# PSUM place of the one-hot products, the sums of w1, the logits, the gated additions and the gates' load in a gated expert block

## The chip, the cores and the metric

The kernel runs on one core of a Trainium2 chip. The metric is the device time of one execution in microseconds (us), lower is better. Before the change it is 282.3 us, the median of three runs (282.22 to 282.58).

A core has five engines with a queue each: PE (TensorE, matrix products into PSUM), DVE (VectorE), ACT (ScalarE), POOL (GpSimd) and SP (SyncE, which here only issues DMAs). Each engine works through its queue in order, and waits where an instruction needs what another engine has not finished.

## The reference

Two gated blocks over x, which has 2048 tokens of 512 numbers. The first sends each token through the one of four experts that its id names; all three matrices of an expert are the same 512x512 matrix. The second is a feed-forward of three layers whose result is added up by routes.

```
x = x + tanh(g_xattn) * xattn(layernorm(x))
x = x + tanh(g_ffn) * ffn(layernorm(x))

xattn(h): e = min(clip(id) // 6250, 3);  y = (silu(h @ C_e.T) * (h @ C_e.T)) @ C_e
ffn(h):   p = softmax(h @ wr.T);  i1, i2 = top_2(p);  gates = p[i] / sum(p[i])
          v = silu(silu(h @ w1.T) @ w3.T) @ w2.T
          out[i_k[t]] += gates[t, k] * v[t]
```

The routes are row numbers from 0 to 7, so the second block changes only the first eight rows of the output: all tokens' v, weighted, are summed into them.

## The kernel before

**Passes.** The tokens are sorted by expert and packed into 17 passes of 128 rows; 13 passes have one expert, four ("shared" passes) have four groups of 32 rows, each with an expert matrix of its own. `order` fixes their sequence, in which the shared passes are the 7th, 11th, 14th and 17th. The place of each token comes from counts that are taken on the chip: `idt` is loaded and compared with the experts' bounds, TensorE counts (`cnt`), DVE works out places, and 16 products of one-hot matrices (`atlane` and `what`) give `tok`, the number of the token at each place (lines 276 to 280). `from_row` and `to_row` are read off `tok` by DVE: the first at once (line 307), the second in `row_tables` (lines 316 and 317), which stands in DVE's queue after the first pass's norms and before the first pass's `g` (line 475). `busy` fills TensorE's waits with products nobody reads.

**One pass.** `gather` (POOL, an indirect DMA) brings 128 rows of x; `load` (SP) brings the expert's matrix of 1 MB, whose number SP first reads from the table `which`; `centre` and `scale` norm the rows on DVE; `turn_in` transposes them on TensorE (`tp_a`) and ACT copies the result; `up` is the first product (z), ACT's Silu and DVE's product (line 475) make `g`; `turn_mid` transposes g (`tp_g`); `down` is the second product (y), which DVE adds to x (line 489) with `tg`, the tanh of the gates; POOL scatters the rows to the output. `norms` norms them again for the feed-forward (small DVE steps on 128x1 and then `h_f`, line 513), `turn_out` transposes them (`tp_f`) into `hT2`.

**The feed-forward.** It runs over two blocks of 1024 rows. The first layer multiplies w1 by hT2 in Strassen's way with seven products in place of eight, and needs sums of parts of w1 (`sums_of_w1`, lines 589 to 592, on POOL) and of hT2 (`sums_of_hT`, on DVE), which also issues the `logits` and transposes them (`turned`). `route` finds the two largest logits and writes the gates `g`, on a tile that POOL clears (line 577). `second_layer(b, g)` covers a quarter of 512 rows: for each of four tiles the product v (line 734), then ACT's Silu into `s2`; then the four additions `acc` (line 746), each a product of a 32-column part of g with s2 into a 32-row part of one PSUM bank. The quarters are numbered 0 to 3. For the last the order is another, since its end is the kernel's end.

**What sets the order.** The program is written in the order in which each engine runs it; nothing reorders it. The main loop (lines 863 to 893) issues pass i's first product, pass i-1's second and pass i-2's last transposes. The feed-forward is a Python generator that issues a piece of work at each `yield`; `step()` takes the next piece, two or so in each pass of the loop, and after the loop all the rest. So TensorE's queue mixes the passes' products with pieces of the feed-forward.

**PSUM and buffers.** There are eight banks: two for tag "mm" (cnt, idle, tok, z, y, v), two for tag "x" (lg and X), one for Y, two for transposes (`tp`), one for the sums (`acc`). A tile of a tag takes the buffer of the one two before it, once that has been read for the last time. Of SBUF, the tiles named in `on_the_way` lie in a pool that is closed after `row_tables`, and its room is used again by the feed-forward's tiles.

Of the kernel before, what the change touches and what calls it, by code (L numbers as in the profile page):

```python
# [8 lines left out]
F32 = mybir.dt.float32  # L9
# [4 lines left out]
AF = mybir.ActivationFunctionType  # L14
# [5 lines left out]
P = 128  # L20
# [5 lines left out]
def tile_gated_moe_ffn(  # L26
# [40 lines left out]
    nc = tc.nc  # L67
# [6 lines left out]
    NP = NJ + 1  # L74
# [4 lines left out]
    NB = NT // TB  # L79
    HB = TB // 2  # L80
    TT = HB // P
# [14 lines left out]
    pos = positions.enter_context(tc.tile_pool(name="pos", bufs=1))  # L96
    on_the_way = {
        "lane", "atlane12", "atlane4", "passes", "what", "place", "over", "rank_in", "incl",
        "keep", "cum", "hot", "before", "later", "stepped", "behind",
    }  # L100

    def ct_(shape, dtype, name):
# [5 lines left out]
    idt = ct_([P, NJ], I32, "idt")  # L108
    nc.sync.dma_start(idt, ids)
    gates = ct_([P, 2], F32, "gates")  # L110
    nc.scalar.dma_start(gates[:, 0:1], g_xattn.to_broadcast([P, 1]))
    nc.scalar.dma_start(gates[:, 1:2], g_ffn.to_broadcast([P, 1]))

    def load_w(src, name):
        w = ct_([P, KC, src.shape[1]], F32, name)
# [62 lines left out]
    for e in range(NR):  # L178
        nc.gpsimd.memset(rank[:, :, e : e + 1], float(NR - e))
    tg = ct_([P, 2], F32, "tg")  # L180
    nc.scalar.activation(tg, gates, AF.Silu)
    nc.scalar.activation(tg, gates, AF.Tanh)


    nc.vector.tensor_tensor(
# [87 lines left out]
        what, what, number.unsqueeze(1).to_broadcast([P, NP, NJ]), ALU.mult  # L273
    )
    at_lane(1)
    tok = ps_mm.tile([P, NP], F32, tag="mm", name="tok")
    for j in range(NJ):
        nc.tensor.matmul(
            tok, atlane[j // H][:, :, j % H], what[:, :, j], start=(j == 0), stop=(j == NJ - 1)
# [158 lines left out]
    def load(p):  # L438

        n0, n = (p, 1) if p < NF else (NF + (p - NF) * G, G)  # L440
        mats[p] = []
        for i in range(n0, n0 + n):
            at = nc.values_load(
                early[i] if i in early else which[0:1, i : i + 1],
                engines=[SP],
                min_val=0,
                max_val=(E - 1) * D,
                skip_runtime_bounds_check_because="an expert's number, times D",
            )
            m = mp.tile([P, KC, D], F32, tag="m", name=f"m_{i}")  # L450
            nc.sync.dma_start(m, ctxT[bass.ds(at, D), :].rearrange("(k p) f -> p k f", p=P))
            mats[p].append(m)
# [130 lines left out]
    def sums_of_w1():  # L583

        h = D // 2
        a11, a12 = w1[:, 0:2, 0:h], w1[:, 2:4, 0:h]
        a21, a22 = w1[:, 0:2, h:D], w1[:, 2:4, h:D]
        ss = [ffp.tile([P, 2, h], F32, tag=f"S{i}", name=f"S{i}") for i in range(1, 5)]
        nc.gpsimd.tensor_add(ss[0], a21, a22)
        nc.gpsimd.tensor_sub(ss[1], ss[0], a11)  # L590
        nc.gpsimd.tensor_sub(ss[2], a11, a21)
        nc.gpsimd.tensor_sub(ss[3], a12, ss[1])
        return a11, a12, a22, ss

    def sums_of_hT(b):

# [128 lines left out]
    def second_layer(b, g):  # L725

        c_b = b % 2 * HB

        def gated(t, half=None):

            c0, n = (0, D) if half is None else (half * D // 2, D // 2)
            v = ps_mm.tile([P, n], F32, tag="mm", name=f"v_{b}_{t}_{c0}")
            for k in range(KC):
                nc.tensor.matmul(  # L734
                    v,
                    s1[:, k, c_b + t * P : c_b + (t + 1) * P],
                    w3[:, k, c0 : c0 + n],
                    start=(k == 0),
                    stop=(k == KC - 1),
                )  # L740
            s2 = work.tile([P, n], F32, tag="s2", bufs=4, name=f"s2_{b}_{t}_{c0}")
            nc.scalar.activation(s2, v, AF.Silu)  # L742
            return s2

        def add(t, s2):
            nc.tensor.matmul(  # L746
                acc[t * Q : (t + 1) * Q, :],
                g[:, t, :],
                s2,
                start=(b == 0),  # L750
                stop=(b == NH - 1 if t < TT - 2 else b == NH - 2),
            )

        def add_turned(t, k, s2):

            nc.tensor.matmul(  # L756
                accT[:, k, :],
                s2,
                g[:, t, 0:NR],
                start=(t == TT - 2 and k == 0),  # L760
                stop=(t == TT - 1 and k == KC - 1),
                skip_group_check=True,
            )

        s2s = []
        if b < NH - 1:
            for t in range(TT):
                s2s.append(gated(t))
                yield
            for t in range(TT):  # L770
                add(t, s2s[t])
            yield SHORT
            return
        for t in range(TT - 1):
            s2s.append(gated(t))
            yield
        for t in range(TT - 2):
            add(t, s2s[t])
        a = work.tile([P, D], F32, tag="g", bufs=2, name="a")
        nc.scalar.copy(a, acc)  # L780
        half0 = gated(TT - 1, 0)
        for k in range(KC):
            add_turned(TT - 2, k, s2s[TT - 2][:, k * P : (k + 1) * P])
        tp = transposed(a, "sum")
        nc.vector.tensor_reduce(
            aT[:, :, 0:NR],
            tp.rearrange("p (k t q) -> p k q t", k=KC, t=TT)[:, :, 0:NR, :],
            AX.X,
            ALU.add,
        )  # L790
        def finish(i, s2):
            n = KC // 2
            for k in range(n):
                add_turned(TT - 1, i * n + k, s2[:, k * P : (k + 1) * P])
            ks = slice(i * n, (i + 1) * n)
            nc.vector.tensor_add(aT[:, ks, 0:NR], aT[:, ks, 0:NR], accT[:, ks, :])

        finish(0, half0)
        half1 = gated(TT - 1, 1)
        out_product(0, KC // 2)  # L800
        finish(1, half1)
# [17 lines left out]

    SHORT = 1  # L820
    last = {b: max(i for i, p in enumerate(order) if min(p // (TB // P), NB - 1) == b) for b in range(NB)}
    running, hT_sums, lts = [], {}, {}

    def step():
        if running:
# [13 lines left out]
    for i in range(1, 5):  # L839
        gather(order[i])  # L840
    load(order[1])
    first_in(order[0])
    centre(order[1])
    scale(order[0], order[1])
# [11 lines left out]
    up(order[1], inside=lambda: turn_mid(order[0]))  # L856
    turn_in(order[2])
    centre(order[3])
    down(order[0])
    turn_mid(order[1])  # L860
    norms(order[3], order[0])
    load(order[4])
    for i in range(2, NP + 2):
        if i < NP:
            up(order[i])
        if i + 1 < NP:
            turn_in(order[i + 1])
        if i + 2 < NP:
            centre(order[i + 2])
        if i + 3 < NP:  # L870
            gather(order[i + 3])
            load(order[i + 3])
        if i <= NP:
            down(order[i - 1])
        else:
            step()
        turn_out(order[i - 2])
        if i <= NP:
            norms(order[i + 2] if i + 2 < NP else None, order[i - 1])
        step()  # L880
        for b in range(NB):
            if last[b] == i - 2:
                hT_sums[b] = sums_of_hT(b)
                running.append(ffn(b))
        if i == 4:
            w1_sums = sums_of_w1()
        if i == 7:
            w3 = load_w(w3T, "w3")
            w2 = load_w(w2T, "w2")
        if i < NP:  # L890
            turn_mid(order[i])
        if last[0] != i - 2:
            step()
    fetched = False
# [52 lines left out]
```

## Time and profile before

| what | value |
|---|---|
| median of three runs | 282.3 us |
| profiled execution | 284.29 us |
| its span (first to last instruction) | 282.6 us |
| granted TensorE clock | 1.0 of full |
| TensorE, a 128x512 f32 product of v, records each | 570 ns, starts 0.43 us apart |
| DVE, T's sums, 128x1024 f32 | 1.22 us |
| POOL, w1's sums, 128x512 f32, four | 1.27 to 1.30 us each |
| ACT, Silu of v, 128x512 | 0.60 us |

The profile comes from one execution, so its span is set against its own 284.29 us. Records of one engine's matrix products overlap[...]: what a product costs is the distance between starts, not a record's length, and "PE busy" can be high where TensorE is held up. In the timeline a row has start, length, engine, line, operation, output and inputs, shape, count, and in brackets the idle time before it with what ended it.

### The profile page before, as it was taken

How to read it: one execution, taken by the hardware profiler on the slowest of the kernel's cores; microseconds unless marked ns; L12 is line 12 of the kernel's file. 1: busy time of each engine (PE TensorE's matmuls, PEld its weight loads, DVE VectorE, ACT ScalarE, POOL GpSimd, SP SyncE). 2: the span in 40 equal slices, each digit the busy share in tenths (PEclk: the TensorE clock that was granted, in tenths of full speed). 3: DMA queues.
4: the chain of work that ended last, by engine and by line, in shares of the span. 5: the costliest groups of instructions: out<-in, count | busy, mean ns of one | idle time of the engine just before them, and what ended most of it. 6: DMA issues, size and time to landing. Idle time of an engine off the chain costs nothing.

```text
span 282.6 us, 3568 instructions
## 1 busy us (share of the span) xinstructions
PE 270.3 (96%) x1173; PEld 126.3 (45%) x1173; DVE 149.0 (53%) x592; ACT 69.5 (25%) x134; POOL 44.3 (16%) x66
## 2 busy tenths in 40 slices
PE   4978999999999999999999999999999999999994
PEld 1434555544445445444444354534345544443463
DVE  4378777799777669935534382506350711620000
ACT  2022213313313321323315132312113224211120
POOL 5420122282222112311101010101010000000000
PEclk9999999999999999999999999999999999999999
DMA  0686999556649998397515085001000000000000
GB/s 1 195 288 196 376 393 382 211 199 224 202 146 396 392 394 333 103 355 258 179 31 186 2 248 232 37 0 39 0 11 0 3 1 0 0 0 2 0 0 2
DMA packets 20722, 42.54 MB, mean 151 GB/s; under 512 B 2143, under 2 KB 2207, under 8 KB 20704
## 3 DMA queue, kind: packets, MB, share of 16 engines
q1 hardware_dynamic: 17664, 33.66, 34.1%
q0 software_dynamic: 2720, 8.65, 8.4%
q8 instruction: 9, 0.15, 0.2%
q14 instruction: 9, 0.07, 0.1%
q10 hardware_dynamic: 320, 0.01, 0.1%
HBM read 38.10 MB, written 4.47 MB: 151 GB/s over the span
## 4 chain that ended last, share of the span: by engine, by line
PE 87%; DVE 7%; DMA 3%; issue 1%; ACT 0%; ACTq 0%; POOL 0%; DVEq 0%
PE y L461 20%; PE v L734 20%; PE z L461 19%; PE X L626 10%; PE Y L626 5%; PE tp_g L388 3%; PE tp_f L388 3%; PE Z L626 2%; PE tp_a L388 2%; DMA x<-in_x_dram,from_row 2%; PE acc L746 1%; DMA idt<-in_ids_dram 1%; PE lg L703 1%; DVE q_f L369 1%; PE accT L756 1%
## 5 line engine op out<-in xcount | busy, mean ns | idle before, releaser
L461 PE MATMUL z<-m,hT 128*32 128x512 f32 (+1 forms) x232 | 61.8, 595 | 2.1 <-DVE pads L320 1.9
L461 PE MATMUL y<-m,gT 128*32 128x512 f32 (+1 forms) x232 | 61.4, 594 | 0.0
L734 PE MATMUL v<-w,s 128*128 128x512 f32 (+1 forms) x136 | 57.0, 570 | 0.0
L734 PEld LDWEIGHTS v<-w,s 128*128 128x128 f32 x136 | 25.1, 190 | 28.2 <-issue 26.8
L461 PEld LDWEIGHTS z<-m,hT 128*32 128x32 f32 (+1 forms) x232 | 22.6, 146 | 31.3 <-issue 27.9
L461 PEld LDWEIGHTS y<-m,gT 128*32 128x32 f32 (+1 forms) x232 | 22.5, 146 | 27.9 <-issue 27.9
L490 POOL DMA_INDIRECT out_dram<-x,to_row x17 | 17.1, 1008 | 90.9 <-DVE x L489 89.0
L397 POOL DMA_INDIRECT x<-in_x_dram,from_row x17 | 16.9, 995 | 72.3 <-DVE h_a L409 29.9
L475 DVE SCALAR_TENSOR_TENSOR g<-z,rs_a,g 128x512 f32<-128x512 f32 x17 | 12.7, 748 | 27.4 <-ACT g L474 27.4
L474 ACT ACTIVATE g<-z,rs_a 128x512 f32<-128x512 f32 x17 | 11.7, 688 | 49.4 <-PE z L461 48.9
L489 DVE SCALAR_TENSOR_TENSOR x<-y,tg,x 128x512 f32<-128x512 f32 x17 | 12.7, 749 | 19.4 <-PE y L461 19.4
L742 ACT ACTIVATE s<-v 128x512 f32<-128x512 f32 (+1 forms) x17 | 9.7, 572 | 44.0 <-PE v L734 44.0
L523 ACT COPY hT<-tp_f 128x512 f32<-128x512 f32 x13 | 7.6, 586 | 43.4 <-PE tp_f L388 43.4
L626 PE MATMUL X<-T,S 128*128 128x512 f32 x32 | 15.0, 592 | 0.0
L348 DVE BATCH_NORM_STATS2 st_a<-x 128x6 f32<-128x512 f32 x16 | 11.0, 686 | 6.6 <-DMA x<-in_x_dram,from_row 6.6
L388 PEld LDWEIGHTS tp_f<-ident,h_f 128*128 128x128 f32 x68 | 8.1, 141 | 11.0 <-issue 9.7
L481 ACT COPY gT<-tp_g 128x512 f32<-128x512 f32 x17 | 10.0, 586 | 12.5 <-PE tp_g L388 12.4
L348 DVE BATCH_NORM_STATS2 st_f<-x 128x6 f32<-128x512 f32 x17 | 11.8, 694 | 0.6
L388 PEld LDWEIGHTS tp_a<-ident,h_a 128*128 128x128 f32 x64 | 7.7, 141 | 9.5 <-issue 9.3
L644 DVE TENSOR_TENSOR s<-X,c 128x512 f32<-128x512 f32 x4 | 2.8, 692 | 16.2 <-PE X L626 16.2
L388 PE MATMUL tp_f<-ident,h_f 128*128 128x128 f32 x68 | 10.5, 276 | 0.6 <-DVE h_f L513 0.6
L388 PE MATMUL tp_g<-ident,g 128*128 128x128 f32 x68 | 10.5, 275 | 0.2
(164 smaller groups left out, 281.6 us busy)
## 6 DMA issues: line engine op xcount, KB each, us to landing
m<-in_ctxT_dram SPq DMA_DIRECT2D x29, 1024.0 KB
w<-in_w1T_dram SPq DMA_DIRECT2D x1, 1024.0 KB
w<-in_w3T_dram SPq DMA_DIRECT2D x1, 1024.0 KB
w<-in_w2T_dram SPq DMA_DIRECT2D x1, 1024.0 KB
x<-in_x_dram,from_row POOLq DMA_INDIRECT x17, 6.3
out_dram<-x,to_row POOLq DMA_INDIRECT x17, 6.0
wr<-in_wrT_dram SPq DMA_DIRECT2D x1, 64.0 KB
x_first<-out_dram SPq DMA_DIRECT2D x4, 4.0 KB
```

The lines of the kernel that those rows point to most:

```text
L348: nc.vector.bn_stats(st, xt)
L388: nc.tensor.transpose(tp[:, k * P : (k + 1) * P], h[:, k * P : (k + 1) * P], ident)
L397: nc.gpsimd.indirect_dma_start(out=xt, out_offset=None, in_=x, in_offset=bass.IndirectOffsetOnAxis(ap=from_row[:, p : p + 1], axis=0),)
L461: nc.tensor.matmul(out_ps[i * n : (i + 1) * n, :], lhs[:, k * P + i * n : k * P + (i + 1) * n], m[:, k, :], start=(k == 0), stop=(k == KC ...
L474: nc.scalar.activation(g, z, AF.Silu, scale=rs)
L475: nc.vector.scalar_tensor_tensor(g, z, rs, g, ALU.mult, ALU.mult)
L481: nc.scalar.copy(gT, tp)
L489: nc.vector.scalar_tensor_tensor(xt, y, tg[:, 0:1], xt, ALU.mult, ALU.add)
L490: nc.gpsimd.indirect_dma_start(out=out, out_offset=bass.IndirectOffsetOnAxis(ap=to_row[:, p : p + 1], axis=0), in_=xt, in_offset=None, bou ...
L626: nc.tensor.matmul(out_ps, a[:, k, c * P : (c + 1) * P], bb[:, k, :], start=start and k == 0, stop=k == 1, skip_group_check=True,)
L734: nc.tensor.matmul(v, s1[:, k, c_b + t * P : c_b + (t + 1) * P], w3[:, k, c0 : c0 + n], start=(k == 0), stop=(k == KC - 1),)
L742: nc.scalar.activation(s2, v, AF.Silu)
```

## The change

- `tok` is taken from the two banks of tag "x" and not from those of tag "mm".
- The gates are loaded on SP's queue, after the matrix of the second pass, and not on ACT's at the program's start. ACT's first instruction, which also loads its function table, reads a tile of ones; the Tanh of the gates comes after the copy of the third pass's transposes.
- The four sums of w1 are issued on DVE, one at the end of each of the loop's rounds 5 to 8, after `norms`, and not together on POOL in round 4.
- `sums_of_hT`, with the logits, is issued after `turn_mid` in a round and not before. This moves the first block's logits behind `tp_g`.
- A quarter's four additions are kept in `owed` and issued after the first v of the next quarter (`pay`). `s2` has five buffers and not four.
- In the last round the piece of the feed-forward that stood before the last `turn_out` comes after it, so the last `tp_f` runs before the second quarter's last v.
- Nine more small tiles lie in the pool that is closed early.

On TensorE the instructions are the same ones, in another order; DVE has four more, POOL four fewer, ACT two DMA issues fewer and SP two more.

```diff
--- before.py
+++ after.py
@@ -96,7 +96,8 @@
     pos = positions.enter_context(tc.tile_pool(name="pos", bufs=1))
     on_the_way = {
         "lane", "atlane12", "atlane4", "passes", "what", "place", "over", "rank_in", "incl",
-        "keep", "cum", "hot", "before", "later", "stepped", "behind",
+        "keep", "cum", "hot", "before", "later", "stepped", "behind", "ones", "place0", "number",
+        "idt", "pad", "psum", "padded", "lanes", "inpass",
     }
 
     def ct_(shape, dtype, name):
@@ -108,8 +109,6 @@
     idt = ct_([P, NJ], I32, "idt")
     nc.sync.dma_start(idt, ids)
     gates = ct_([P, 2], F32, "gates")
-    nc.scalar.dma_start(gates[:, 0:1], g_xattn.to_broadcast([P, 1]))
-    nc.scalar.dma_start(gates[:, 1:2], g_ffn.to_broadcast([P, 1]))
 
     def load_w(src, name):
         w = ct_([P, KC, src.shape[1]], F32, name)
@@ -178,8 +177,7 @@
     for e in range(NR):
         nc.gpsimd.memset(rank[:, :, e : e + 1], float(NR - e))
     tg = ct_([P, 2], F32, "tg")
-    nc.scalar.activation(tg, gates, AF.Silu)
-    nc.scalar.activation(tg, gates, AF.Tanh)
+    nc.scalar.activation(tg, ones_f[:, 0:2], AF.Silu)
 
 
     nc.vector.tensor_tensor(
@@ -273,7 +271,7 @@
         what, what, number.unsqueeze(1).to_broadcast([P, NP, NJ]), ALU.mult
     )
     at_lane(1)
-    tok = ps_mm.tile([P, NP], F32, tag="mm", name="tok")
+    tok = ps_x.tile([P, NP], F32, tag="x", name="tok")
     for j in range(NJ):
         nc.tensor.matmul(
             tok, atlane[j // H][:, :, j % H], what[:, :, j], start=(j == 0), stop=(j == NJ - 1)
@@ -586,11 +584,15 @@
         a11, a12 = w1[:, 0:2, 0:h], w1[:, 2:4, 0:h]
         a21, a22 = w1[:, 0:2, h:D], w1[:, 2:4, h:D]
         ss = [ffp.tile([P, 2, h], F32, tag=f"S{i}", name=f"S{i}") for i in range(1, 5)]
-        nc.gpsimd.tensor_add(ss[0], a21, a22)
-        nc.gpsimd.tensor_sub(ss[1], ss[0], a11)
-        nc.gpsimd.tensor_sub(ss[2], a11, a21)
-        nc.gpsimd.tensor_sub(ss[3], a12, ss[1])
-        return a11, a12, a22, ss
+        w1_sums.extend((a11, a12, a22, ss))
+        nc.vector.tensor_add(ss[0], a21, a22)
+        yield
+        nc.vector.tensor_sub(ss[1], ss[0], a11)
+        yield
+        nc.vector.tensor_sub(ss[2], a11, a21)
+        yield
+        nc.vector.tensor_sub(ss[3], a12, ss[1])
+        yield
 
     def sums_of_hT(b):
 
@@ -738,7 +740,7 @@
                     start=(k == 0),
                     stop=(k == KC - 1),
                 )
-            s2 = work.tile([P, n], F32, tag="s2", bufs=4, name=f"s2_{b}_{t}_{c0}")
+            s2 = work.tile([P, n], F32, tag="s2", bufs=5, name=f"s2_{b}_{t}_{c0}")
             nc.scalar.activation(s2, v, AF.Silu)
             return s2
 
@@ -751,6 +753,12 @@
                 stop=(b == NH - 1 if t < TT - 2 else b == NH - 2),
             )
 
+        def pay():
+
+            for f, t, s2 in owed:
+                f(t, s2)
+            owed.clear()
+
         def add_turned(t, k, s2):
 
             nc.tensor.matmul(
@@ -766,13 +774,15 @@
         if b < NH - 1:
             for t in range(TT):
                 s2s.append(gated(t))
+                if t == 0:
+                    pay()
                 yield
-            for t in range(TT):
-                add(t, s2s[t])
-            yield SHORT
+            owed.extend((add, t, s2s[t]) for t in range(TT))
             return
         for t in range(TT - 1):
             s2s.append(gated(t))
+            if t == 0:
+                pay()
             yield
         for t in range(TT - 2):
             add(t, s2s[t])
@@ -819,7 +829,7 @@
 
     SHORT = 1
     last = {b: max(i for i, p in enumerate(order) if min(p // (TB // P), NB - 1) == b) for b in range(NB)}
-    running, hT_sums, lts = [], {}, {}
+    running, hT_sums, lts, w1_sums = [], {}, {}, []
 
     def step():
         if running:
@@ -839,6 +849,8 @@
     for i in range(1, 5):
         gather(order[i])
     load(order[1])
+    nc.sync.dma_start(gates[:, 0:1], g_xattn.to_broadcast([P, 1]))
+    nc.sync.dma_start(gates[:, 1:2], g_ffn.to_broadcast([P, 1]))
     first_in(order[0])
     centre(order[1])
     scale(order[0], order[1])
@@ -856,10 +868,13 @@
     up(order[1], inside=lambda: turn_mid(order[0]))
     turn_in(order[2])
     centre(order[3])
+    nc.scalar.activation(tg, gates, AF.Tanh)
     down(order[0])
     turn_mid(order[1])
     norms(order[3], order[0])
     load(order[4])
+    summing = sums_of_w1()
+    owed = []
     for i in range(2, NP + 2):
         if i < NP:
             up(order[i])
@@ -872,23 +887,23 @@
             load(order[i + 3])
         if i <= NP:
             down(order[i - 1])
-        else:
-            step()
         turn_out(order[i - 2])
         if i <= NP:
             norms(order[i + 2] if i + 2 < NP else None, order[i - 1])
         step()
-        for b in range(NB):
-            if last[b] == i - 2:
-                hT_sums[b] = sums_of_hT(b)
-                running.append(ffn(b))
-        if i == 4:
-            w1_sums = sums_of_w1()
+        if i > NP:
+            step()
+        if 5 <= i < 9:
+            next(summing)
         if i == 7:
             w3 = load_w(w3T, "w3")
             w2 = load_w(w2T, "w2")
         if i < NP:
             turn_mid(order[i])
+        for b in range(NB):
+            if last[b] == i - 2:
+                hT_sums[b] = sums_of_hT(b)
+                running.append(ffn(b))
         if last[0] != i - 2:
             step()
     fetched = False
```

## The prediction

> **What bounds the kernel now.** I read the shares by engine first, then the chain of waits, then the timeline of each stretch where TensorE's starts are further apart than its own work.
>
> ```profile
> PE 270.3 (96%) x1173; PEld 126.3 (45%) x1173; DVE 149.0 (53%) x592; ACT 69.5 (25%) x134; POOL 44.3 (16%) x66
> PE 87%; DVE 7%; DMA 3%; issue 1%; ACT 0%; ACTq 0%; POOL 0%; DVEq 0%
> ```
>
> TensorE carries the end, and nothing in the change removes a product: its instructions before and after are the same, in another order. So only holes can be gained. A 128x512 f32 product is eight records 0.43 us apart (3.44 us in the chain), so a hole is whatever exceeds that pitch. The timeline has six places; first the start and the fifth pass:
>
> ```profile
> 3.63 0.21 DVE L185 TENSOR_TENSOR cum<-idt,bounds 128x48 bf16<-128x48 int32 x1 [2.03 <-DMA idt<-in_ids_dram]
> 21.94 0.18 DVE L317 SCALAR_TENSOR_TENSOR to_row<-tok,pad 128x17 int32<-128x17 f32 x1
> 22.22 2.81 PE L461 MATMUL z<-m,hT 128*128 128x512 f32 x6 [1.88 <-DVE pads L320]
> 23.07 0.74 DVE L475 SCALAR_TENSOR_TENSOR g<-z,rs_a,g 128x512 f32<-128x512 f32 x1
> 24.87 0.60 PE L388 MATMUL tp_g<-ident,g 128*128 128x128 f32 x4
> ...
> 56.46 1.83 DVE L369 SCALAR_TENSOR_TENSOR q_f<-r_f,v_f 128x1 f32<-128x1 f32 x1
> 56.97 1.30 POOL L589 TENSOR_TENSOR S<-w 128x512 f32<-128x512 f32 x1
> 63.06 0.63 PE L388 MATMUL tp_f<-ident,h_f 128*128 128x128 f32 x4 [0.57 <-DVE h_f L513]
> ```
>
> z of the second pass idles 1.88 us until the row tables have read tok for the last time (to_row, 22.12): z takes tok's PSUM buffer. At 56 to 62 us the small DVE steps of a norm stretch from 0.22 to 1.83 us while GpSimd sums w1, and tp_f comes late. Then the logits and the gated additions:
>
> ```profile
> 105.61 2.44 PE L703 MATMUL lg<-hT,wr 128*32 128x128 f32 x62
> 108.35 0.38 PE L703 MATMUL lg<-hT,wr 128*32 128x128 f32 x2 [0.31 <-issue]
> 108.66 1.00 PE L388 MATMUL tp_g<-ident,g 128*128 128x128 f32 x4
> ...
> 196.88 0.60 ACT L742 ACTIVATE s<-v 128x512 f32<-128x512 f32 x1 [2.85 <-PE v L734]
> 197.22 1.37 PE L746 MATMUL acc<-s,g 128*32 128x512 f32 x8
> ...
> 217.04 1.43 PE L746 MATMUL acc<-s,g 128*32 128x512 f32 x8
> 217.92 2.29 PE L703 MATMUL lg<-hT,wr 128*32 128x128 f32 x64
> 220.29 1.98 PE L626 MATMUL X<-hT,w 128*128 128x512 f32 x4
> ...
> 258.26 1.80 PE L746 MATMUL acc<-s,g 128*32 128x512 f32 x8
> 258.36 0.60 ACT L742 ACTIVATE s<-v 128x512 f32<-128x512 f32 x1 [2.84 <-PE v L734]
> ```
>
> At 197 and 258 the four additions start while ScalarE is still making the last s2 that they need; at 217 they do not, and take 0.84 us up to the next product's first load.
>
> [...]
>
> **The change part by part** (us of the profiled execution, 284.29 with a span of 282.6; the median of the unprofiled runs is 282.3, so the same sum is taken from 282.3.)
>
> 1. *tok in ps_x.* z of the second pass no longer waits for to_row. It can start when the first z ends and hT is copied, at about 20.2 (hT: 19.51+0.59); its matrix is in by then, as the DMA share is 0.43 in 19 to 21 us and 0.02 in 21 to 23. But after six of its eight records (2.58 us, so 22.8) stands tp_g, which needs g of DVE, done at 23.81 behind the row tables whose order does not change. So tp_g starts at 23.9 and not 24.87: 1.0 gained of 1.9, the next wait is g. h_a of the third pass (24.66+0.49=25.15) is just in time for its transposes, then at 25.2. Further on there is room: x's DVE step at 30.24 waits 0.99 on y, and z of the third pass at 30.48 has its matrix issued at 22.31. -1.0; ends -0.5 and -1.05.
>
> 2. *Gates later, on SP's queue.* Beside idt, two 128-row broadcasts leave the DMA engines; idt's landing heads the whole start (it is the first 2.79 us of the chain), and everything up to z, the matrices' and x's loads included, follows it. The trace does not show idt alone: bounds 0 and -0.5 (a quarter of DVE's 2.03 us wait), I take -0.2. On SP the two issues (0.41 and 0.45 us before) come between the second and third matrix, where SP waits 9.6 us for the table anyhow: nothing. They queue behind the second matrix, in the DMA lull of 21 to 23 us. ScalarE's Silu on ones only loads the table sooner; Tanh (0.20) goes in front of a gT copy, with ScalarE 25% busy: nothing. What waits behind it is in the slow rival.
>
> 3. *w1's sums on DVE, one in each of four passes.* POOL loses 5.1 us. From y's start to the next z's it was 58.90 to 64.28 = 5.38 us; one pass earlier 50.71 to 55.02 = 4.31. -1.07, taken as -1.05; ends -0.8 and -1.1. Added: four DVE sums, [...]. Each stands between h_f and g, where DVE idles 0.84 to 0.89 us for ScalarE in the passes at 77.0, 85.5 and 93.7: hidden. Were it not, g has over 3 us until tp_g. Cost 0 (at most 0.2). [...]
>
> 4. *First logits behind tp_g.* 105.61 to the next z at 109.49 is 3.88 us; the work is 16 rounds of four column groups at 0.109 = 1.75, and 0.44 of tp_g: 1.7 lost, in the last six logits and in tp_g, put down to "issue". No wait for data is seen, so hiding ScalarE's copy behind tp_g hides nothing that is shown. I take -0.2; ends +0.2 and -1.6.
>
> 5. *Additions owed to the next quarter.* 197.22 to 198.51 is 1.29 us against 0.84: -0.45. 258.26 to 259.99 is 1.73: -0.85 (0.04 left for a change of weights' width). Ends of both -0.9 and -1.35. The fifth s2 buffer lets the next v be evacuated before the additions; without it that activation would wait for them. The POOL memset of g (two buffers) now waits for the owed additions until about 245, with nothing behind it on POOL but the last memset; g itself is finished at 259.9 before, so nothing.
>
> 6. *Last block.* The last tp_f goes ahead of the quarter's last v, so ScalarE's four copies (217.26 to 218.76) and T's first sum (218.79) lie beside 3.44 us of product, and the logits find everything there. From 216.51, tp_f to X is 3.78 us; tp_f 0.53, additions 0.84, logits 1.75 to 2.0 make 3.1 to 3.4. -0.6 of it; ends -0.3 and -0.7.
>
> Sum: 1.0+0.2+1.05+0.2+0.45+0.85+0.6 = 4.35. Profiled 284.3 to about 279.9; median 282.3 to 278.0. What binds then is TensorE's own pitch from 20 us on; DMA is not next, as the loads wait for TensorE (102.7 us of SP's waits are for y).
>
> **The rivals.**
> - *The stall of the logits is a lack of time ahead of them* and goes once tp_g stands there, and idt gains its 0.5: 1.4+0.3 more, 276.3. For it: the second logits, in a stretch almost without DMA, take 2.0 us and not 2.9. Against: tp_g, in front or behind, brings only 0.44 us.
> - *The start and the last block give little*: the second matrix lands after 21.3, or g decides more than I see, and X still waits for the transposed logits behind T on DVE (0.35 before). Then 1.0+0.2 and 0.3 to 0.4 fall away: 279.4. Against: DMA share 0.02 from 21 us on.
> - *Slower: the gates come too late.* Tanh stands in ScalarE's queue before the second gT copy; behind it waits y of the second pass on TensorE, and x's sum of the first on DVE. After the gains y is due near 33.1, so with 0.2 for Tanh and 0.6 for the copy every us of landing after 32.3 costs one, and from 36.7 on the 4.35 are gone. Behind the matrices that SP issues until then, say a landing at 38, it gives 283.6. Against: their place is before those matrices, and by ScalarE's wait the second had landed 3.4 us after its issue.
> - *That the sums do not stop the contention* [...]: gathers have slack, DVE's wait for x is 6.6 us over five; at worst part 3 is halved, 278.5, inside my range.
>
> **How the numbers follow.** Forecast 278.0, chance 0.70, own range 277.0 to 279.0 (ends of parts 1, 2, 4 and 6 not all at once). 276.3 gets 0.13, 279.4 gets 0.13, slower 0.03; 0.01 for no change. The range takes in both fast rivals, since either alone left out brings the rest near two in ten: 276.2 to 279.5. This measurement tells 0.2% (0.6 us) from no change; faster 0.96, same 0.01, slower 0.03.
>
> **What would show it.** Right: z of the second pass near 20.2 with tp_g about 1 us earlier and a wait for g; no DVE step of 128x1 above 0.4 us and no wait of tp_f at 60 to 62; additions of 0.86 us in both quarters; X after the logits without a wait for lt. Undecided and to be read: the gap in the first logits, idt's landing, the length of S on DVE. Wrong if a g or tp_g in passes six to nine waits on DVE, if Tanh waits on the gates with gT behind it, or if a loss at the start is made up nowhere because z waits for a matrix.

## The result, and the profile after

The changed kernel takes 278.5 us (median of 4 runs, 277.82 to 278.80) where the kernel before, run beside it, takes 282.26 us (4 runs, 281.75 to 282.58). The ratio is 0.9865, with a 95% interval of 0.9842 to 0.9889. Forecast were 278.0 us, range 276.2 to 279.5. So the timed gain is 3.8 us, and by the interval 3.1 to 4.5; the prediction's sum is 4.35. The profiled execution took 278.80 us, its span is 277.1 us.

The page of the profile after: busy shares (the first line) and the shares of the chain that ended last.

```profile
PE 267.2 (96%) x1173; PEld 125.2 (45%) x1173; DVE 147.3 (53%) x596; ACT 69.2 (25%) x134; POOL 39.1 (14%) x62
...
PE 91%; DVE 4%; DMA 3%; issue 1%; POOL 0%; DVEq 0%
```

TensorE has the same 1173 products and a larger share of the chain (91% where it was 87%); GpSimd has four instructions and 5.2 us less. Now the places that the prediction named, in the timeline of after (start, length, engine, line, operation, in brackets the idle time and what ended it). First the start:

```profile
2.48 0.21 DVE L183 TENSOR_TENSOR cum<-idt,bounds 128x48 bf16<-128x48 int32 x1 [0.86 <-DMA idt<-in_ids_dram]
...
18.65 3.68 PE L459 MATMUL z<-m,hT 128*128 128x512 f32 x8
...
21.30 0.18 DVE L315 SCALAR_TENSOR_TENSOR to_row<-tok,pad 128x17 int32<-128x17 f32 x1
...
22.43 0.74 DVE L473 SCALAR_TENSOR_TENSOR g<-z,rs_a,g 128x512 f32<-128x512 f32 x1
...
23.32 0.63 PE L386 MATMUL tp_g<-ident,g 128*128 128x128 f32 x4 [0.99 <-DVE g L473]
```

z of the second pass runs on without a hole, and the next wait is g behind the row tables, as foreseen. But the count on idt (`cum`) starts at 2.48 us and not at 3.63, a gain of which only a small part had been foreseen. Then the first logits, and the end of the second quarter:

```profile
102.61 0.60 PE L386 MATMUL tp_f<-ident,h_f 128*128 128x128 f32 x4
103.05 0.60 PE L386 MATMUL tp_g<-ident,g 128*128 128x128 f32 x4
103.58 1.95 PE L705 MATMUL lg<-hT,wr 128*32 128x128 f32 x64
105.46 1.12 PE L459 MATMUL z<-m,hT 128*128 128x512 f32 x2
...
208.51 0.60 PE L386 MATMUL tp_f<-ident,h_f 128*128 128x128 f32 x4
...
208.95 3.60 PE L736 MATMUL v<-w,s 128*128 128x512 f32 x8
...
212.48 1.95 PE L705 MATMUL lg<-hT,wr 128*32 128x128 f32 x64
...
214.36 1.98 PE L628 MATMUL X<-hT,w 128*128 128x512 f32 x4
```

From the last tp_f before the first logits to the z after them it is 2.85 us, and was 4.41 us in the profile that the prediction was made from. X follows the second logits without a wait. The three sets of additions, at 196.72, 242.03 and 256.95 us, each stand in front of another quarter's product; the second of them:

```profile
242.03 1.06 PE L748 MATMUL acc<-s,g 128*32 128x512 f32 x8
...
243.02 2.41 PE L736 MATMUL v<-w,s 128*128 128x512 f32 x5
```

From its start to the next product's it is 0.99 us (the third, from 256.95 to 257.95: 1.00 us). The unhindered additions of before, at 217.04, took 0.88 us by this measure; the prediction's 0.84 us ended at the next product's weight load.

### The profile page after: what moved, and what is told of

It is laid out like the page before. It is cut to its first block, busy times and chain, and to the rows that moved or that the text cites. A ratio compares the mean times of both kernels' runs of the same rounds, so it can differ in the third digit from the quotient of the medians.

```text
span 277.1 us, 3564 instructions
## 1 busy us (share of the span) xinstructions
PE 267.2 (96%) x1173; PEld 125.2 (45%) x1173; DVE 147.3 (53%) x596; ACT 69.2 (25%) x134; POOL 39.1 (14%) x62
## 4 chain that ended last, share of the span: by engine, by line
PE 91%; DVE 4%; DMA 3%; issue 1%; POOL 0%; DVEq 0%
PE y L459 21%; PE v L736 20%; PE z L459 19%; PE X L628 10%; PE Y L628 5%; PE tp_f L386 3%; PE tp_g L386 3%; PE tp_a L386 3%; PE Z L628 2%; DMA x<-in_x_dram,from_row 2%; PE acc L748 1%; PE lg L705 1%; PE accT L764 1%; DMA idt<-in_ids_dram 1%; PE o L820 0%
## 5 line engine op out<-in xcount | busy, mean ns | idle before, releaser
L386 PEld LDWEIGHTS tp_g<-ident,g 128*128 128x128 f32 x68 | 8.2, 141 | 5.5 <-issue 5.2
```

The lines of the kernel that those rows point to most:

```text
L386: nc.tensor.transpose(tp[:, k * P : (k + 1) * P], h[:, k * P : (k + 1) * P], ident)
```

## The experiments

Twelve kernels were run, in three sets of four; each set ran on one chip beside the kernel before, whose median was 282.6, 283.48 and 282.43 us. The profiles differ in two things that no edit explains: the time from the issue of the second pass's gather to its first norm step (4.8 to 6.7 us), and a hole of 1.4 to 1.8 us in the first logits, which some executions have. Of the sets, the second has the longest gathers, three of the four holes and the slowest runs of the kernel before, so its medians stand about 1 us higher and are to be read by their ratios. The intervals of most ratios reach 0.3 to 0.5% to each side, about 1 us, so parts of the change are told apart by stretches of the trace: a stretch that an edit doesn't touch has the same length within 0.1 us in almost every profile (the exceptions, in undo_sums and gates_later, are named there).

**The kernel before, once more (before_again).**

> The kernel before, unchanged. The first profile of it took 284.29 us while the timed runs took 282.3, and 1.7 us of that profile lie in the first logits, in waits put down to 'issue'. Theory: that stall belongs to that one execution; then the first logits here take 1.8 to 2.1 us up to tp_g, not 3.05, the profiled execution takes 282.3 to 282.8, and the gain in the timed runs (3.8 us) is the sum of the trace's gains (5.5) without the 1.56 seen there. Rival: the stall comes with the order (logits ahead of tp_g); then it is here again, 1.0 us or more, and the profiled execution is again near 284.

282.93 us, ratio 1.0008 (0.9993 to 1.0023); profiled 282.19 us, span 280.5 us. The same stretch with the first logits:

```profile
104.49 0.60 PE L388 MATMUL tp_f<-ident,h_f 128*128 128x128 f32 x4
...
105.02 1.96 PE L703 MATMUL lg<-hT,wr 128*32 128x128 f32 x64
...
107.40 3.17 PE L461 MATMUL z<-m,hT 128*128 128x512 f32 x7
```

2.91 us, with the logits in the old place: the 1.5 us that the prediction saw lost there were of that execution and not of the order. The expectation's theory held. This profile is the fairer base. Beside it stands a second profile of after (below), with nearly the same gather:

| stretch (us) | before_again | after_again | gained | forecast |
|---|---|---|---|---|
| start to `cum` (idt has landed) | 3.62 | 2.67 | 0.95 | 0.2 |
| `cum` to the issue of the second gather | 8.16 | 8.18 | 0.0 | |
| that issue to its first norm step | 4.90 | 4.88 | 0.0 | |
| norm step to the first tp_g | 7.62 | 6.68 | 0.94 | 1.0 |
| first tp_g to the fifth | 29.71 | 29.79 | -0.1 | |
| fifth to sixth (w1's sums) | 9.13 | 8.18 | 0.95 | 1.05 |
| sixth tp_g to tp_f before the logits | 41.35 | 41.33 | 0.0 | |
| that tp_f to the next z | 2.91 | 2.85 | 0.06 | 0.2 |
| that z to the 15th tp_f | 83.32 | 83.42 | -0.1 | |
| 15th tp_f to the last sums' turn (`accT`) | 80.48 | 78.95 | 1.53 | 1.90 |
| rest | 9.29 | 9.27 | 0.0 | |
| span | 280.49 | 276.20 | 4.29 | 4.35 |

The gather's row is in the sum: with another pair of profiles it would move the total by up to 1.9 us, while each other row that an edit doesn't touch stays within about 0.2 us, but for the hole. The two rows of -0.1 us belong to edits: the first is 29.71 us in the three profiles with tok in "mm" and 29.73 to 29.79 in eight with tok moved, the second 83.32 wherever the logits stand ahead of tp_g and 83.42 wherever they stand behind it in one piece.

The experiments that follow undo one part each in the changed kernel. Their stretches, where they differ from after_again's:

| kernel | start to `cum` | gather | norm to tp_g | fifth to sixth | to the logits | logits | tail | span |
|---|---|---|---|---|---|---|---|---|
| after_again | 2.67 | 4.88 | 6.68 | 8.18 | 41.33 | 2.85 | 78.95 | 276.20 |
| undo_tok | 2.56 | 5.14 | **7.60** | 8.18 | 41.34 | 2.85 | 78.95 | 277.32 |
| undo_gates | **3.83** | 5.37 | 6.69 | 8.18 | 41.33 | 2.85 | 78.94 | 277.98 |
| undo_logits | 2.46 | 5.70 | 6.69 | 8.18 | 41.33 | **2.91** | 78.95 | 276.72 |
| undo_sums | 2.66 | 5.21 | 6.69 | **9.39** | 42.35 | 2.85 | 78.94 | 278.73 |
| undo_owed | 2.54 | 6.73 | 6.69 | 8.18 | 41.33 | 4.57 | **80.71** | 281.37 |
| undo_last | 2.57 | 6.51 | 6.69 | 8.19 | 41.32 | 4.61 | **80.32** | 280.91 |

"Gather" is the row from issue to first norm step, "tail" the one from the 15th tp_f to accT; bold is the stretch that the edit touches. The two spans of 281 us are not the price of their edits: 1.6 to 1.9 us of each is the gather and 1.7 to 1.8 us the hole in the logits, neither of which the edit touches.

**tok back in tag "mm" (undo_tok).**

```diff
-    tok = ps_x.tile([P, NP], F32, tag="x", name="tok")
+    tok = ps_mm.tile([P, NP], F32, tag="mm", name="tok")
```

> The changed kernel with tok in the two banks of tag mm again. Theory: z of the second pass waits for to_row at about 21.5 us, tp_g comes 0.9 us later than in the changed kernel (24.2, not 23.3): 279.4. Rival (z's early start is eaten by g): 278.5, tp_g at 23.3.

279.23 us, ratio 0.9885 (0.9839 to 0.9931). The timeline of undo_tok:

```profile
20.67 0.18 DVE L315 SCALAR_TENSOR_TENSOR to_row<-tok,pad 128x17 int32<-128x17 f32 x1
...
20.95 2.81 PE L459 MATMUL z<-m,hT 128*128 128x512 f32 x6 [1.63 <-DVE pads L318]
...
23.60 0.60 PE L386 MATMUL tp_g<-ident,g 128*128 128x128 f32 x4
```

The old wait is back, as the theory had it (the view names `pads`, DVE's next instruction, which overlaps the end of to_row). Since the row tables hang on the gather and so on chance, the clean measure starts at the end of to_row: from there to tp_g it is 2.75 us here (23.60 less 20.85), 2.75 in both profiles of before, and 1.84 in after (23.32 less 21.48). The move is worth 0.91 us at tp_g, of which 0.07 is lost again by the fifth (29.71 and 29.78 us, above). In the times undo_tok's median is 0.96 us over that of undo_logits, which ran in the same set and whose edit is worth nothing (below).

**The gates at the start again, on ACT's queue (undo_gates).**

```diff
+    nc.scalar.dma_start(gates[:, 0:1], g_xattn.to_broadcast([P, 1]))
+    nc.scalar.dma_start(gates[:, 1:2], g_ffn.to_broadcast([P, 1]))
...
-    nc.scalar.activation(tg, ones_f[:, 0:2], AF.Silu)
+    nc.scalar.activation(tg, gates, AF.Silu)
+    nc.scalar.activation(tg, gates, AF.Tanh)
```

The loads on SP and the later Tanh are left out.

> The changed kernel with both gates loaded on ACT's queue at the start and Silu and Tanh of them there, as before. Theory: the broadcasts slow idt by 1.16 us (first count on TensorE at 4.12 us, not 2.96), but half of that is lost again since the second gather's rows come later with the gates' packets on SP's queue; so it costs 0.6 to 0.7 us: 279.1. The second gather's norm then starts 5.4 us after its issue, not 6.0. Rival: all of 1.16 counts: 279.7. Second rival: idt's landing is hidden: 278.5.

279.37 us, ratio 0.9861 (0.9828 to 0.9894): the timed ratio can't tell this from after; the median is 1.1 us over that of undo_logits from the same set, and the trace shows the place. cum comes at 3.83 us. The view of the DMA of the first 5 us, in 40 slices of 0.125 us, of undo_gates:

```profile
DMA  0000000000000000000111111110000000000000
GB/s 0 0 0 0 0 0 0 0 0 0 0 0 0 0 0 0 0 1 3 12 11 5 7 6 8 10 7 0 0 1 0 0 0 0 0 1 0 0 0 0
...
q10 hardware_dynamic: 288, 0.00, 2.6%
q1 hardware_dynamic: 144, 0.01, 1.9%
```

and of after:

```profile
DMA  0000000000000003200000000000000000000000
GB/s 0 0 0 0 0 0 0 0 0 0 0 0 0 0 6 38 22 0 0 0 0 0 0 0 0 0 0 0 0 0 0 0 0 0 0 0 0 0 0 0
DMA packets 144, 0.01 MB, mean 2 GB/s; under 512 B 144, under 2 KB 144, under 8 KB 144
```

idt's 144 packets alone (q1) pass in about three slices. With the gates' 288 packets of a few bytes beside them (q10) the two pass together in about ten slices, and begin three later. In the kernel before, with the same two loads at the start, the view of 2.2 to 3.3 us counts 131 packets of q1 and 128 of q10: the two go by nearly one for one. The pace falls too: these 259 packets take 1.1 us, while in after the view of 1.8 to 2.2 us has all 144 within 0.3 us. Why is open. Whether one large load beside idt would cost as much was not run. In all eleven profiles without these loads at the start, cum is at 2.46 to 2.67 us, in the three with them at 3.62 to 3.83. From cum to the second gather's issue it is 8.1 to 8.3 us in all of them: the 0.95 to 1.4 us goes down to there whole, and the later stretches of undo_gates are those of after_again but for the gather. The gather takes 5.37 us here, as expected, but 4.81 to 6.73 us in the ten profiles with the gates behind the second matrix. So the theory's half that is lost again through the gather isn't shown; against its first rival (all of it counts) it stays undecided.

**The first logits ahead of tp_g (undo_logits).** The call of `sums_of_hT` is put back ahead of `turn_mid`.

> The changed kernel with the first block's logits ahead of tp_g again, nothing else undone. Theory (the stall was of one execution, the order is worth nothing): within 0.3 us of the changed kernel's 278.5, from tp_f's start to the next z's about 2.8 us as in the changed kernel. Rival (the order makes the stall): 280.0, with gaps of 0.3 to 0.6 us among the last logits.

278.27 us, ratio 0.9833 (0.9799 to 0.9867), no slower than after. The timeline of undo_logits:

```profile
102.28 0.60 PE L386 MATMUL tp_f<-ident,h_f 128*128 128x128 f32 x4
...
105.19 2.31 PE L459 MATMUL z<-m,hT 128*128 128x512 f32 x5
```

The stretch is 2.91 us against 2.85, but the one after it is 83.32 against 83.42: the 0.06 us that the order gives are lost again, and the theory (worth nothing) held.

**w1's sums on POOL, in round 4 (undo_sums).**

```diff
-        nc.vector.tensor_add(ss[0], a21, a22)
-        yield
+        nc.gpsimd.tensor_add(ss[0], a21, a22)
...
-        if 5 <= i < 9:
-            next(summing)
+        if i == 4:
+            sums_of_w1()
```

(The other three sums likewise.)

> The changed kernel with w1's four sums on POOL again, in round 4. Theory: [...] (between tp_g of the 5th and of the 6th pass 9.1 us, not 8.2), so 279.3 against 278.4 for the changed kernel. Rival (the sums on DVE give back a part): 278.9 or less while the trace still shows 0.95.

280.34 us, ratio 0.9873 (0.9837 to 0.9910). The timeline of undo_sums:

```profile
55.08 1.65 DVE L373 TENSOR_TENSOR r_f<-r_f,w_f 128x1 f32<-128x1 f32 x1
...
55.39 1.30 POOL L588 TENSOR_TENSOR S<-w 128x512 f32<-128x512 f32 x1
...
61.23 0.63 PE L386 MATMUL tp_f<-ident,h_f 128*128 128x128 f32 x4 [0.82 <-DVE h_f L511]
```

The stretched steps and tp_f's wait are back, and the pass is 1.21 us longer, where 0.95 was expected; nothing of it is given back. The other 1.0 us of this profile lies in a shared pass's z some 35 us later, 4.64 us where 3.64 is usual. The view puts 0.86 us of it down to a wait for the pass's matrix (DMA); why that came late isn't known. gates_later, with the sums on DVE, has 4.28 us there, so it is not put to the edit. In after tp_f of the fifth pass has no wait, no DVE step of 128x1 is longer than 0.4 us, and the sums cost nothing:

```profile
60.85 0.60 PE L386 MATMUL tp_f<-ident,h_f 128*128 128x128 f32 x4
...
73.62 0.69 DVE L590 TENSOR_TENSOR S<-S,w 128x512 f32<-128x512 f32 x1
...
74.55 0.75 DVE L473 SCALAR_TENSOR_TENSOR g<-z,rs_a,g 128x512 f32<-128x512 f32 x1 [0.24 <-ACT g L472]
```

g behind this sum still waits 0.24 us for ScalarE, and behind the first and third 0.40 and 0.28. Behind the fourth it follows at once, and tp_g comes 3.3 us later without a wait. So the 0.69 us are hidden.

**The additions at their quarter's end (undo_owed), and the last tp_f behind v (undo_last).** Of undo_owed and then of undo_last:

```diff
-            owed.extend((add, t, s2s[t]) for t in range(TT))
+            for t in range(TT):
+                add(t, s2s[t])
+            yield SHORT
```

```diff
+        else:
+            step()
         turn_out(order[i - 2])
...
-        if i > NP:
-            step()
```

> The changed kernel with each quarter's additions straight after its own four v's, the last tp_f still ahead of the last v. Theory: in each of three quarters they wait for the Silu of the last v, 0.45 us at the first, 0.75 at the second (which has no tp_f or tp_g ahead of it now) and 0.75 at the third, less 0.1 each for fewer changes of weights' width: 280.1. Rival (as the prediction summed it, only two quarters): 279.6.

> The changed kernel with the last tp_f after the second quarter's last v again, the additions still owed. Theory: now nothing stands between tp_f and the logits; ScalarE's four copies take 2.2 us after tp_f, the second half of the logits waits for them about 1.2 us, and T's first sum keeps the logits' transposes from X for 0.3 more: 279.8. So the two edits are worth more together than the prediction's 0.6. Rival (0.6 as predicted): 279.0.

281.75 us, ratio 0.9925 (0.9893 to 0.9958), and 282.06 us, ratio 0.9935 (0.9906 to 0.9964). The tails are 80.71 and 80.32 us; with both edits undone it is 80.48 (before_again), with both made 78.95. So each of them alone brings +0.16 us (the additions, undo_last) or -0.23 us (the last tp_f, undo_owed), and both together 1.53 us. By the tails undoing costs 1.76 and 1.37 us, which is what the two theories put beside 278.4 (1.7 and 1.4). The timed medians lie higher still. That fits the hole that both profiles have; up to the hole both programs are after's, so neither edit makes it.

The two meet in one place, the stretch from the 16th tp_f to X:

| kernel | 15th to 16th tp_f | 16th tp_f to X | X to accT |
|---|---|---|---|
| before_again (neither) | 12.90 | 14.57 | 53.01 |
| undo_last (additions alone) | 12.27 | 14.58 | 53.47 |
| undo_owed (last tp_f alone) | 12.90 | 14.80 | 53.01 |
| after_again (both) | 12.27 | 13.21 | 53.47 |

The first and third column hang on the additions alone. In the second, undo_last gains nothing though the second quarter's additions, 0.88 us, have left it for the third column. The timeline of undo_owed:

```profile
212.06 3.60 PE L736 MATMUL v<-w,s 128*128 128x512 f32 x8
...
215.59 1.37 PE L748 MATMUL acc<-s,g 128*32 128x512 f32 x7
215.70 0.60 ACT L744 ACTIVATE s<-v 128x512 f32<-128x512 f32 x1 [1.83 <-PE v L736]
...
216.48 0.60 PE L705 MATMUL lg<-hT,wr 128*32 128x128 f32 x10
...
216.81 0.59 PE L748 MATMUL acc<-s,g 128*32 128x512 f32 x1
```

With tp_f gone ahead, the additions stand right behind the v whose Silu they need. And of undo_last:

```profile
214.38 0.60 PE L386 MATMUL tp_f<-ident,h_f 128*128 128x128 f32 x4
...
214.91 2.83 PE L705 MATMUL lg<-hT,wr 128*32 128x128 f32 x64
...
216.66 1.22 DVE L604 TENSOR_TENSOR T<-hT 128x1024 f32<-128x1024 f32 x1 [8.76 <-ACT hT L533]
...
218.16 1.98 PE L628 MATMUL X<-hT,w 128*128 128x512 f32 x4 [0.42 <-DVE lt L716]
```

With the additions gone, nothing is left between tp_f and the logits, which now meet ScalarE's four copies (2.83 us where 1.95 is usual), and X waits for lt behind T. Each of the two pieces was the other's cover.

**The gates behind more matrices (gates_later): the rival that was to be slower.**

```diff
     load(order[1])
-    nc.sync.dma_start(gates[:, 0:1], g_xattn.to_broadcast([P, 1]))
-    nc.sync.dma_start(gates[:, 1:2], g_ffn.to_broadcast([P, 1]))
...
     wr = load_w(wrT, "wr")
+    nc.sync.dma_start(gates[:, 0:1], g_xattn.to_broadcast([P, 1]))
+    nc.sync.dma_start(gates[:, 1:2], g_ffn.to_broadcast([P, 1]))
```

> The changed kernel with the gates' two loads on SP after wr, not after the second matrix. Theory: their packets no longer run beside the second gather, whose rows then come 5.0 to 5.2 us after its issue and not 5.7 to 6.0, and 0.3 to 0.5 us of the start is gained: 278.0. Rival: the second gather's time is set by the 1 MB matrix that runs beside it; 5.7 to 6.0 as before and 278.4.

282.02 us, ratio 0.9939 (0.9914 to 0.9965). Theory and rival of the expectation missed by some 4 us: both spoke of the second gather alone (it took 6.11 us) and overlooked the wait that the prediction's slow rival had described. The timeline of gates_later:

```profile
24.55 0.49 SPq L860 DMA_DIRECT2D gates<-in_g_ffn_dram  x1
...
33.33 0.20 ACT L871 ACTIVATE tg<-gates 128x2 f32<-128x2 f32 x1 [7.00 <-DMA gates<-in_g_ffn_dram]
...
33.56 0.75 DVE L487 SCALAR_TENSOR_TENSOR x<-y,tg,x 128x512 f32<-128x512 f32 x1 [4.89 <-ACT tg L871]
...
34.46 1.96 PE L459 MATMUL y<-m,gT 128*128 128x512 f32 x4 [1.11 <-DVE x L487]
```

The second load of half a kilobyte lands 8.8 us after its issue, behind 2 MB of matrices in the same queue. Tanh waits, gT's copy and y behind it, as the rival had it. From the first tp_g to the fifth it is 31.31 us and not 29.79, so 1.5 us are lost for a landing at 33.3; the rival's rule (one us for each after 32.3) gives 1.0. The span is 4.8 us longer than after_again's; the other 3.3 us lie elsewhere, 1.2 in the gather, 0.6 in a shared pass's z (4.28 us) and 1.4 in the hole of the logits. In after itself Tanh runs at 25.90 us without a wait.

**The changed kernel again, and three edits on top.** after_again, split_logits (of the first block, the second half's logits behind the next z), tables_later, and both edits together (both):

```diff
-        lgs = [logits(b, half) for half in range(2)]
+        lgs = [logits(b, half) for half in range(1 if b == 0 else 2)]
...
+        if last[0] == i - 3:
+            lts[0].append(turned(0, 1, logits(0, 1)))
```

```diff
-    row_tables()
-    positions.close()
-    ffp = ctx.enter_context(tc.tile_pool(name="ffp", bufs=1))
     up(order[0], inside=lambda: turn_in(order[1]))
...
     up(order[1], inside=lambda: turn_mid(order[0]))
+    row_tables()
+    positions.close()
+    ffp = ctx.enter_context(tc.tile_pool(name="ffp", bufs=1))
```

> The changed kernel as it is, beside the three below. If the 1.5 us that the first logits lose in some executions is chance in either order, this profile may show it or not: from the last tp_f before the logits to the z after them 2.9 us without it, 4.3 to 4.6 with it. Theory: 278.3 us timed, tp_g of the first pass near 23.3 us, its wait 0.5 to 1.0 on g. Rival (moving tp_g ahead of the logits cures the stall): 2.9 us here and in split_logits alike.

> After, but of the first block the second half's logits stand behind the next pass's first product, not right after the first half's. Theory [...]: with two bursts of 64 no gap above 0.2 us in either, the stretch costs 2.9 us as in an execution without the stall; the median falls at most 0.3 us under after_again's, and the spread of its times is smaller. Rival (the stall comes of the DMA traffic beside it, not of the length of the burst): gaps of 0.3 us or more in one of the two halves in some executions, spread as before.

> After, but the row tables stand on DVE behind g of the second pass, not ahead of g of the first. Theory (with tok out of z's way, g on DVE behind the row tables is what tp_g of the first pass waits for): g starts near 21.1 and not 22.4, tp_g's wait of 0.99 us on g is gone or under 0.2, tp_g starts 0.7 to 1.0 us earlier for the same start of the first z, and the end follows: 277.4 to 277.7 us where after is 278.3. Rival (something else, such as the third pass's matrix or rows, is next, and takes the gain back by 31 us): the same time as after within 0.2 us.

> The edits of split_logits and tables_later together. Theory: their gains add, 277.2 to 277.6 us, below both kernels of the change. Rival: 278.3, as after.

| kernel | median, range (us), 6 runs each | ratio to before, 95% | span of the profile |
|---|---|---|---|
| after_again | 278.09, 277.78 to 279.61 | 0.9858, 0.9827 to 0.9888 | 276.2 |
| split_logits | 278.33, 277.88 to 278.97 | 0.9849, 0.9825 to 0.9874 | 277.1 |
| tables_later | 277.72, 276.95 to 278.46 | 0.9833, 0.9806 to 0.9859 | 275.3 |
| both | 277.44, 277.27 to 278.23 | 0.9826, 0.9802 to 0.9851 | 275.6 |

The wait that the change uncovered can be removed too. The timeline of tables_later:

```profile
20.11 0.74 DVE L473 SCALAR_TENSOR_TENSOR g<-z,rs_a,g 128x512 f32<-128x512 f32 x1
...
21.53 0.60 PE L386 MATMUL tp_g<-ident,g 128*128 128x128 f32 x4
...
24.74 0.18 DVE L315 SCALAR_TENSOR_TENSOR to_row<-tok,pad 128x17 int32<-128x17 f32 x1
```

tp_g waits for nothing; from the norm step to it are 5.90 us and not 6.68, 0.78 gained, and nothing takes it back by the end of the span. In the times it is 0.4 to 0.65 us of median with intervals that overlap, so the trace shows the gain and the times only lean to it. The medians of tables_later and both lie in the ranges expected for them, that of both without the gain it was to have from the split.

split_logits was to be a little faster than after_again and is not. It issues the first block's logits in two bursts of 64 instructions (32 products and 32 weight loads) and not in one of 128. Whether the length of a burst has to do with the hole was the author's guess, and these runs decide nothing: the hole is in none of the four profiles, split or not. The split itself costs: logits and the stretch after them are 87.22 us (2.63 and 84.59) in split_logits and 86.56 in both, against 86.27 whole. In split_logits z, then due earlier, waits 0.59 us for its matrix. Where the hole does occur it looks like this (undo_owed):

```profile
103.81 0.60 PE L386 MATMUL tp_g<-ident,g 128*128 128x128 f32 x4
...
104.33 2.08 PE L705 MATMUL lg<-hT,wr 128*32 128x128 f32 x53
...
106.79 0.41 PE L705 MATMUL lg<-hT,wr 128*32 128x128 f32 x3 [0.38 <-issue]
...
107.52 0.49 PE L705 MATMUL lg<-hT,wr 128*32 128x128 f32 x8 [0.32 <-issue]
```

tp_g stands ahead and the hole is there all the same: neither order of the two cures it.

## Why the prediction was right, and which terms were not

The sum was 4.35 us and the fair pair of profiles shows 4.29. The total is as near as that by luck, since two errors cancel: the gates were taken 0.75 us too low, the other terms 0.7 us too high together. What was read of tok and of w1's sums held, the gates and the additions were mis-sized, and the logits' term was a share of a chance delay. The timed gain of 3.8 us is lower than both sums, but its interval takes both in.

1. *tok, 1.0 forecast, 0.91 measured at tp_g, 0.85 by the fifth.* The step holds as it was put: z free, g behind the row tables next, tp_g later than z alone would allow. The two other conditions (matrix and third pass in time) held.
2. *Gates, 0.2 forecast with ends 0 and 0.5; 0.95 to 1.4 measured.* The one term whose ends missed. "A quarter of DVE's 2.03 us wait" had no reading behind it. The DMA view of before would have given a hint: idt's 144 packets lie among the gates' 288, from 2.2 to 3.3 us 131 of the one beside 128 of the other. An estimate from that (half of 1.1 us) would still have been low. That all up to z follows idt was right, and the second load's place was harmless, as said. ACT's table load (1.28 us) begins at 0.81 us in after and at 4.68 in before, sooner as said. gates_later shows that the slower rival was a real one, decided by two matrices in the queue.
3. *w1's sums, 1.05 forecast, 0.95 measured, 1.2 by undoing it.* The cause is shown in both directions: with the sums on POOL, small DVE steps beside them take up to 1.83 us (before) and 1.65 us (undo_sums); with the sums on DVE none is above 0.4 us (after). How the two engines hold each other up is not shown. The length of a sum on DVE was the author's estimate, with no run behind it. In after a sum takes 0.683 to 0.686 us, and it is hidden where it was said to be.
4. *Logits, 0.2 forecast, 0.06 measured, and lost again behind them.* The prediction found no reason for the hole in the edit and took 0.2 of its 1.7 us. Even that was too much: the hole is missing from a second profile of the kernel before, and there in three later ones with tp_g in front. So the first rival, by which time ahead of the logits would end it, falls.
5. *Additions, 1.3 forecast, and 6. the last block, 0.6; together 1.53 measured.* By place (the table above): the first quarter 0.63 (forecast 0.45), of which 0.42 is the additions themselves, 1.30 us before and 0.88 after. With the second quarter's 0.88 us counted where they went, the last block 0.48 (forecast 0.6) and the rest 0.42 (forecast 0.85). Most mis-sized is the 0.85. The third set of additions does gain 0.73 us (from 1.73 to 1.00), but the second set costs 0.11 us more in its new place (0.99 for 0.88), and the 56 records of v in that stretch take 24.52 us for 24.33, as the additions now cut their run once more. From v to the additions, and from them back to v, the weights change between 128 and 32 columns, and there the starts are 0.52 us apart (before and after alike) where those of v are 0.43. The sum had 0.04 us for all of this. The second error is that the two parts were added up as if independent: in the last block each is worth its gain only if the other is made. The sign "additions of 0.86 us in both quarters" was missed too.

Against the profile that the prediction quotes (span 282.6) after's 277.1 is 5.5 us less; 1.5 us of that is the hole, the gathers differ by 0.55 the other way, and idt gains 0.2 more than in the fair pair.

## What to carry to other kernels

A small load at the head of a program, which all else waits for, was worth keeping alone on the DMA engines: here the other queue's 288 packets cost 0.95 to 1.4 us, though they held only a few bytes. Where such loads went instead, what stood ahead of them in the queue decided here: behind one matrix they were in before Tanh was due at 25.9 us, behind 2 MB more only at 33.3. Two edits of order that remove waits in one place should be priced as one, by writing down what stands between producer and consumer after both. And a hole put down to "issue" in a single profile is to be looked for in a second one before it enters a sum.

## What had not been expected of the hardware

- Two broadcasts of one number to 128 partitions, 288 packets, delay a load of 8 KB by 0.95 to 1.4 us: `cum` comes at 3.62 to 3.83 us with them and at 2.46 to 2.67 without.
- The second pass's gather takes 4.8 to 6.7 us from issue to the first step on its rows, with the same program up to there; it sets when the first tp_g can start. What sets it is open. The gates' place alone does not: it is 4.90 to 5.44 us with them at the start, 4.81 to 6.73 behind the second matrix, 6.11 further back.
- The 64 products of a block's logits start 0.03 us apart, in after in fours 0.11 us apart. In the first block they have a hole of 1.4 to 1.8 us in four of the twelve profiles that issue them in one piece (before, undo_owed, undo_last, gates_later; the last three in one set). The DMA engines are full beside the first (busy share 1.05 in before and undo_owed, which have the hole, and 1.05 in after, which hasn't) and idle beside the second (0.03 to 0.04 in the same three), where no profile has it, so full DMA isn't enough for it; whether it is needed was not shown. Near it something else is longer in two profiles: the 32 narrow products of z in the shared pass just ahead take 3.64 us in twelve profiles, 4.28 in gates_later and 4.64 in undo_sums. The cause of the hole is open.
